# A graph layer on one core: the adds of a gathered pair's sums go to steps 6 and 7 of a block

## The chip, the core and the metric

The kernel runs on one core of a Trainium2 chip. The metric is the time on the device in microseconds (us); lower is better. Times below are of single executions or medians of several, as stated. The engines are called TensorE (PE in the profile, with PEld for its weight loads), VectorE (DVE), ScalarE (ACT), GpSimd (POOL) and SyncE (SP, which issues transfers).

## What is computed

One layer of a graph network over 6250 nodes with 64 features and 206250 edges, which are sorted by their destination:

```python
h = jnp.maximum(_layernorm(x, axis=-1), 0.0)
msg = h[src] + edge_attr_64
agg = jax.ops.segment_sum(msg, dst, num_segments=6250)
y = jax.nn.relu(agg @ W1 + b1) @ W2 + b2
return x + y
```

## The kernel before, in words

All sums `agg` live in one tile on the chip, `sums` in the profile: 128 rows (64 features, in two halves that the first layer's product adds up) and a column for each node. Three things are added into its columns, and then the layers read them.

**Counts.** For most edges `h[src]` isn't fetched. For each destination the kernel counts how often each source occurs, and multiplies the counts with `h`. The nodes are cut into 23 blocks of 252 columns (the last nodes are left to two more sets of layers, 23 and 24), and each block into 14 steps of 6 windows; step n of the whole is step n mod 14 of block n // 14. In a step (`count`) TensorE does 6 products of one-hot tiles (`pc`, line 847) and ScalarE copies them to a ring (`counts`, line 850). The one-hot tiles `hot_lo` and `hot_key` (line 837) are made by VectorE for three steps at once; there are two buffers of each. While block b is counted, the counts of block b - 1 are multiplied with `h` (`pv`, line 866), spread over steps 0 to 6, and `add_products` (line 879) adds them to `sums` at step 10.

**Features of the edges.** `chunk_sum` sums the features of the edges by 48 small products (`bank`, line 434) at steps 7, 10 and 13, from tiles `feat` that SyncE loads two units ahead, into tiles that an earlier sum has freed (line 413); VectorE's one-hot tile for it, `hot` (line 422), is made one step before. Their place among the columns is made by products into `pv` (line 450) at step 3 of the next block.

**Gathered pairs.** The last 18 groups of 1024 edges go another way, two groups at a time, so there are nine pairs, 184 to 200. GpSimd gathers the rows `h[src]` and adds them to the loaded features (`pfeat`, line 296; 16 gathers a pair). When a pair should have landed by the planner's clock, `features_h` sums it by 32 products into `bank` (line 477). A few steps later `place_groups` puts the sums at their columns (`placed`, line 489) and ScalarE copies them to `sum_p` (line 491). Later still `add_sums` adds `sum_p` to `sums` by two VectorE instructions (line 461). The first column is a number that VectorE reads at run time, so the two adds can touch any column: they are ordered against every reader and writer of `sums`.

**Layers.** At step 8 (and 11 where there are enough) `mlp` starts the layers of a block that is complete: `ph` (line 915), the product with W1, in the step itself, with ScalarE's copy `hid` (line 917); `po` (line 922) two steps later, with ScalarE's copy `y` (line 928); the bias onto the rows of `x` (`xs`, line 907) nine steps later, the add to `y` (line 933) ten steps later and the store `out_y` (line 943) on SyncE eleven steps later.

**Checks.** At some steps ScalarE also looks over tiles of indices (`check_nodes`, `check_keys`; `junk` in the profile, line 673): among others at steps 145 and 146 of block 10, and 187 and 188 of block 13.

Each engine's work is written out in order by the Python program: the loop over n calls the work of a step, then what was put down for it with `at`, in the order in which it was put down. Waits between engines are set from the tiles that instructions read and write, in that order. Nothing is scheduled anew behind it.

The step of a pair's adds is found by `add_later`, from the step `n_placed` at which the pair is placed. The steps of the pairs, from the program:

```
pair   summed  placed  adds
184      46      57     62  (block 4, step 6)
186      84      86     91  (block 6, step 7)
188     112     114    119  (block 8, step 7)
190     141     144    149  (block 10, step 9)
192     172     183    188  (block 13, step 6)
194     210     212    217  (block 15, step 7)
196     238     240    245  (block 17, step 7)
198     270     281    286  (block 20, step 6)
200     308     310    313  (block 22, step 5)
```

Of the kernel before, what the change touches and what calls it, by code (L numbers as in the profile page):

```python
# [76 lines left out]
NW = 23  # L77
# [39 lines left out]
def gnn_kernel(ctx: ExitStack, tc: tile.TileContext, x, src_t, dst_t, dst_g, edge, w1, b1, w2, b2, out):  # L117
# [326 lines left out]
    def chunk_place(u):  # L444
        b, c, n = units[u]
        of = by_node.pop(u)
        unplaced[b] -= 1
        for i in range(n):
            a = column(b, (c + i) * CN)
            nc.tensor.matmul(pvs[b][0][i * D:(i + 1) * D, a:a + CN], of[:, i, :], select, start=False, stop=False)  # L450
# [4 lines left out]
    def add_sums():  # L455
        for g, placed in to_add:
            for b in range(GB):
                done_at[g + b] = max(made)
                half = slice(b * D, (b + 1) * D)
                to = agg[half, ds(bases.pop(g + b), W)]  # L460
                nc.vector.tensor_tensor(to, to, placed[half, :], op=OP.add)
        to_add.clear()
# [361 lines left out]
    def count(b, s):  # L824

        t = b * BT + s * ST
        n = b * STEPS + s
        r = n - opens(n)
        if r == 0:
            n = min(ST * (1 if n == 0 else R - 1 if n < R else R), NW * BT - t)  # L830
            assert all(at_col.get(c % KR) == c for c in range(t, t + n)), t
            opened[0] = t + n
            hots[:] = [work.tile([P, R * ST, P], BF16, name="hot_lo"),
                       work.tile([P, R * ST, K + 1], BF16, name="hot_key")]
            for k, (hot, iota_k) in enumerate(zip(hots, (iota_lo, iota_key))):
                m = hot.shape[2] // 2
                nc.vector.tensor_tensor(  # L837
                    hot[:, :n].rearrange("p t (m o) -> p t m o", o=2),
                    iota_k.rearrange("p (m o) -> p m o", o=2).unsqueeze(1).to_broadcast([P, n, m, 2]),
                    keys[:, k, t % KR:t % KR + n, :].unsqueeze(2).to_broadcast([P, n, m, 2]), op=OP.is_equal)  # L840
                if k and 0 < b * STEPS + s < OPEN:
                    nc.vector.memset(spare, 0.0)
        hot_lo, hot_key = (hot[:, r * ST:(r + 1) * ST, :] for hot in hots)
        pc = ps.tile([P, 2, 512], F32, tag="pc", name="pc")
        for j in range(ST):
            k, m = divmod(j, ST // 2)
            nc.tensor.matmul(pc[:, k, m * K:(m + 1) * K], hot_lo[:, j, :], hot_key[:, j, :K],  # L847
                             start=True, stop=True)
        half, i = divmod(s, STEPS // 2)
        nc.scalar.activation(  # L850
            ring[:, (2 * b + half) % 3, :, i * ST * V:(i + 1) * ST * V].rearrange("p h (k m) -> p h k m", k=2),
            pc[:, :, :ST // 2 * K].rearrange("p k (m h) -> p h k m", h=HI), AF.Copy)
# [4 lines left out]
    def multiply(b, upto):  # L857

        if b not in pvs:
            open_pv(b)  # L860
        pv, done = pvs[b]
        assert upto < HI or unplaced[b] == 0
        a, z = sorted(((2 * b) % 3, (2 * b + 1) % 3))
        of = ring[:, a:z + 1:z - a]
        for h in range(done, upto):
            nc.tensor.matmul(pv.rearrange("p (k n) -> p k n", k=2), h2[:, h, :], of[:, :, h, :],  # L866
                             start=(h == 0), stop=(h == HI - 1))
        pvs[b][1] = max(done, upto)
# [3 lines left out]
    def add_products(b):  # L872
        pv, done = pvs.pop(b)[:2]
        assert done == HI
        n = BN - (NX * V if b == SB else 0)
        for a, z in ((0, n),) if 2 * b % 3 != 2 else ((0, NH), (NH, n)):
            to = agg[:, start[b] + a:start[b] + z]
            k = column(b, start[b] + a)
            nc.vector.tensor_tensor(to, to, pv[:, k:k + z - a], op=OP.add)  # L879
        if b == SB:  # L880
            k = column(b, start[b] + n)
            nc.vector.tensor_copy(tail, pv[:, k:k + NX * V])

    def add_seconds(k):
        n = min(4, NX - k)
        node = nc.values_load_multi_w_load_instructions(
            second_n[0:1, k:k + n], engines=[mybir.EngineType.DVE], min_val=0, max_val=DUMP,
            skip_runtime_bounds_check_because="sums of a node's number and 0, at most DUMP by a min")[1]
        for j in range(n):
            to = agg[:, ds(node[j], V)]  # L890
            nc.vector.tensor_tensor(to, to, tail[:, (k + j) * V:(k + j + 1) * V], op=OP.add)
# [4 lines left out]
    def residual(b):  # L896
        if b not in xs:
            xs[b] = late.tile([NP, 2, D], F32, name="xs", bufs=4)
            nc.sync.dma_start(xs[b][:pairs[b]], x[start[b]:start[b + 1], :].rearrange("(p k) d -> p k d", k=2))
# [70 lines left out]
    def pool_until(us):  # L970
        while queue and pool[0] <= us:
            cost, f = queue.pop(0)
            pool[0] += cost
            f()

    def features_h(g):
        read_bases(g, GB)
        sum_groups(g, hot_groups(g), [parts_of.pop(g + b) for b in range(GB)])
        for b in range(GB):
            fetch_h(g + 2 * GB + b)  # L980
# [88 lines left out]
    def clock(n):  # L1069

        return n * HEAD_US if n < STEPS else STEPS * HEAD_US + (n - STEPS) * STEP_US

    steps = [(b, s) for b in range(NW) for s in range(STEPS)]
    first_step = [steps.index((b, 0)) for b in range(NW)]
    last = len(steps)
# [4 lines left out]
    PRODUCTS = (5, 12, 19, 26, 33, 41, HI)  # L1080
    ADDED, LOADED = 10, 2
    LAST, LATE = (5, 10), 9
    GROUPS, PLACED = (0, 1, 2, 4), (1, 2, 4, 5)
    ready = []
    queued = set()
# [2 lines left out]
    def at(step, f, *a):  # L1088
        later.setdefault(step, []).append(lambda: f(*a))

    def mlp(m, n):
        for k, f in ((0, mlp_hidden), (2, mlp_product), (9, bias), (10, mlp_add), (11, mlp_store)):
            at(n + k, f, m)
# [13 lines left out]
    def add_later(n):  # L1107

        upto = h_next

        def f():
            add_sums()
            for m in range(NW, NB):
                if (upto >= G or (start[m + 1] + 30) * (E / N) <= upto * P * J) and m not in queued:
                    queued.add(m)
                    ready.append(m)
        at(n, f)

    for n, (b, s) in enumerate(steps):
        for f in before.get(n, []):  # L1120
            f()
        count(b, s)
        if b >= 1 and s < len(PRODUCTS):
            multiply(b - 1, PRODUCTS[s])
        if b >= 1 and s == PLACES:
            for u in places[b - 1]:
                chunk_place(u)
        if b >= 1 and s == (ADDED if b < NW - 1 else LATE):
            add_products(b - 1)
            if b - 1 > SB:  # L1130
                ready.append(b - 1)
        k = n - (first_step[SB + 1] + ADDED + 1)
        if 0 <= k < 3 * -(-NX // 4) and k % 3 == 0:
            add_seconds(k // 3 * 4)
            if k // 3 == -(-NX // 4) - 1:
                ready[:0] = range(SB + 1)
        if s == LOADED or b == NW - 2 and s == STEPS // 2:
            for m in ready[:len(LAYERS)] if b < NW - 1 else ready + [NW - 2, NW - 1]:
                if m not in xs:
                    residual(m)  # L1140
        if b == NW - 1 and s == STEPS // 2:
            for m in range(NW, NB):
                if m not in queued:
                    residual(m)
        if s in (LAYERS if b < NW - 1 else LAST) and ready and ready[0] in xs:
            mlp(ready.pop(0), n)
        for f in later.pop(n, []):
            f()
        if n >= 3:
            if h_next < G and s in GROUPS and fetched.get(h_next + 1, 1e9) + LAND_US <= clock(n):  # L1150
                features_h(h_next)
                n_placed = next((k for k in range(n + 2, last) if b == NW - 1 or steps[k][1] in PLACED), last)
                at(n_placed, place_groups, h_next)
                h_next += GB
                add_later(next((k for k in range(n_placed + (3 if b == NW - 1 else 5), last) if steps[k][1] != ADDED), last))
            if n == 3:
                pool[0] = clock(n - 1) + OPENING_US
            pool_until(clock(n) + LAND_US)
# [142 lines left out]
```

## Time and profile before

| | |
|---|---|
| three runs without a profile | 478.10, 478.37, 478.75 us; median 478.37 |
| the profiled execution, its own time | 481.19 us |
| its span, first to last instruction | 479.4 us |
| busy: TensorE, VectorE, ScalarE, GpSimd | 418.0, 417.1, 369.0, 355.8 us |

The page and its views are read like this. A row of the order of time has start, length (both us), engine, line, operation, tiles, sizes and number of instructions, and in brackets the engine's idle time before it and what ended that. Neighbouring instructions of the same kind are merged to one row, so a row of 48 products has the length of them all. A row of the table of waits has who waited, for whom, then us in total, times, and the longest. TensorE's granted clock stands in tenths of full speed for 40 equal slices of the span (12 us each), or as a share in a table of stretches. The chain that ended last is followed back from the last instruction, each time to what released it.

### The profile page before, as it was taken

To read this page: it belongs to the slowest core of one execution; us is meant where nothing else is said; L and a number is where in the kernel's file an instruction comes from. 1 tells how busy PE (TensorE), PEld (TensorE's weight loads), DVE (VectorE), ACT (ScalarE), POOL (GpSimd) and SP (SyncE) were. 2 spreads that over 40 slices of the span, in tenths; PEclk is the share of its full clock that TensorE was granted. 3 is DMA by queue.
4 is the path that set the end of the run, shared out by engine and by line. 5 is a ranking of instruction groups with operands and counts; after the bars stand their busy time and mean duration, and the time that the engine had idled before them with its cause. 6 is when DMAs were issued, how large, how long until landed. Compare 5 with 4: busy or idle time off the path is not lost.

```text
span 479.4 us, 17275 instructions
## 1 busy us (share of the span) xinstructions
PE 418.0 (87%) x7339; PEld 373.4 (78%) x7340; DVE 417.1 (87%) x562; ACT 369.0 (77%) x611; POOL 355.8 (74%) x223
## 2 busy tenths in 40 slices
PE   2147698999988999999979999999999999999974
PEld 2136597887887898898878988988988988888964
DVE  7788989889999899989699899898998899898740
ACT  3636889978878789889868789787887788688650
POOL 7777888898888888888888888888888888500000
PEclk9999699999999999999989999999999999999998
DMA  9949457468367668576674694596695694474330
GB/s 236 219 148 313 118 147 167 98 175 218 66 161 193 155 172 228 121 202 166 152 189 114 178 246 105 142 248 142 147 241 123 158 225 106 130 210 133 91 83 16
DMA packets 120050, 77.70 MB, mean 162 GB/s; under 512 B 32448, under 2 KB 118400, under 8 KB 119744
## 3 DMA queue, kind: packets, MB, share of 16 engines
q1 hardware_dynamic: 97452, 67.13, 47.9%
q0 software_dynamic: 22288, 8.67, 14.1%
q8 instruction: 59, 0.97, 0.9%
q10 hardware_dynamic: 228, 0.75, 0.5%
q14 instruction: 23, 0.19, 0.1%
HBM read 72.53 MB, written 3.99 MB: 160 GB/s over the span
## 4 chain that ended last, share of the span: by engine, by line
PE 70%; ACT 11%; DMA 8%; DVE 6%; issue 3%; POOL 1%; DVEq 0%; ACTq 0%; POOLq 0%
PE pv L866 27%; PE pc L847 23%; PE bank L434 10%; ACT counts L850 8%; PE po L922 3%; DMA rows<-in_dst_g,row_i 2%; DMA feat<-in_edge 2%; PE pv L450 2%; DVE hot_key L837 2%; DMA dstq<-in_dst_g,cols_i 2%; DVE hot_lo L837 1%; POOL rows L296 1%; PE ph L915 1%; ACT junk L673 1%; DMA firsts_i<-in_dst_g 1%
## 5 line engine op out<-in xcount | busy, mean ns | idle before, releaser
L296 POOL DMA_INDIRECT pfeat<-table,src_p x144 | 299.7, 2081 | 45.0 <-issue 39.9
L850 ACT ACTIVATE counts<-pc 128x882 fp32r<-128x882 f32 x322 | 286.2, 916 | 56.7 <-PE pc L847 49.9
L847 PE MATMUL pc<-hot_key,hot_lo 128*128 128x147 bf16 x1932 | 180.8, 232 | 27.1 <-ACT counts L850 16.9
L866 PE MATMUL pv<-counts,h 128*128 128x252 f32 x1127 | 171.6, 292 | 0.1
L847 PEld LDWEIGHTS <-hot_lo 128*128 128x128 bf16 x1932 | 132.2, 100 | 49.2 <-issue 22.9
L837 DVE TENSOR_TENSOR hot_key<-iota_key,keys 128x2664 bf16<-128x2664 bf16 (+1 forms) x109 | 165.5, 1519 | 0.0
L837 DVE TENSOR_TENSOR hot_lo<-iota_lo,keys 128x2304 bf16<-128x2304 bf16 (+1 forms) x109 | 145.6, 1336 | 21.4 <-PE pc L847 18.1
L866 PEld LDWEIGHTS pv<-counts,h 128*128 128x128 f32 x1127 | 143.6, 190 | 0.4 <-ACT counts L850 0.3
L434 PE MATMUL bank<-feat,hot 128*21 128x64 f32 x3288 | 62.4, 225 | 0.2 <-DMA feat<-in_edge 0.2
L434 PEld LDWEIGHTS bank<-feat,hot 128*21 128x21 f32 x3288 | 49.9, 103 | 9.5 <-issue 0.7
L422 DVE TENSOR_TENSOR hot<-rel,iota 128x504 f32<-128x504 bf16 x69 | 46.5, 673 | 0.0
L296 POOL DMA_INDIRECT words<-packed,first_i x15 | 21.2, 1413 | 4.6 <-issue 4.3
L296 POOL DMA_INDIRECT rows<-in_dst_g,row_i x15 | 18.7, 1248 | 5.2 <-issue 3.0
L437 ACT ACTIVATE by_node<-bank 128x128 f32<-128x128 f32 x69 | 19.5, 283 | 2.1 <-PE bank L434 1.9
L879 DVE TENSOR_TENSOR sums<-sums,pv 128x126 f32<-128x126 f32 (+2 forms) x31 | 10.0, 343 | 11.0 <-PE pv L866 10.9
L917 ACT ACTIVATE hid<-ph,b1s 128x252 f32<-128x252 f32 (+2 forms) x25 | 11.6, 463 | 9.0 <-PE ph L915 9.0
L922 PE MATMUL po<-w2s,hid 128*126 128x64 f32 (+2 forms) x100 | 17.1, 295 | 1.2 <-ACT hid L917 1.2
L922 PEld LDWEIGHTS po<-w2s,hid 128*126 128x126 f32 (+2 forms) x100 | 13.8, 198 | 4.3 <-ACT hid L917 2.0
L915 PE MATMUL ph<-sums,w1s 128*128 128x252 f32 (+2 forms) x50 | 16.2, 405 | 0.5 <-ACT y L928 0.4
L450 PE MATMUL pv<-select,by_node 128*64 128x42 f32 x274 | 12.6, 235 | 0.0
L450 PEld LDWEIGHTS pv<-select,by_node 128*64 128x64 f32 x274 | 9.9, 137 | 3.1
L312 ACT ACTIVATE inrow<-rows,nhalf 128x256 bf16<-128x256 int32 x15 | 7.4, 499 | 5.2 <-DMA rows<-in_dst_g,row_i 5.2
(201 smaller groups left out, 244.4 us busy)
## 6 DMA issues: line engine op xcount, KB each, us to landing
feat<-in_edge SPq DMA_DIRECT2D x137, 384.0 KB
pfeat<-in_edge SPq DMA_DIRECT2D x18, 256.0 KB
pfeat<-table,src_p POOLq DMA_INDIRECT x144, 4.4
xl<-in_x SPq DMA_DIRECT2D x2, 768.0 KB
xs<-in_x SPq DMA_DIRECT2D x23, 63.0 KB
out_y<-y SPq DMA_DIRECT2D x23, 63.0 KB
dstn<-in_dst_g SPq DMA_DIRECT2D x1, 1024.0 KB
table<-xl SPq DMA_DIRECT2D x1, 800.0 KB
```

Source lines behind the costliest of these rows:

```text
L296: nc.gpsimd.indirect_dma_start(out=rows, out_offset=None, in_=source, in_offset=bass.IndirectOffsetOnAxis(ap=index, axis=0), compute_op=op)
L422: nc.vector.tensor_tensor(hot_of[u][:, :n].rearrange("p c j w -> p (c j) w"), rel[:, c:c + n].rearrange("p c q k -> p (c q k)").unsqueeze( ...
L434: nc.tensor.matmul(bank[q * QP:q * QP + WQ, i * D:(i + 1) * D], hot[:, i, j, :], feat[i][:, j, :], start=(k == 0), stop=(k == JP - 1))
L437: nc.scalar.activation(by_node[u][:, :n].rearrange("p c d -> p (c d)"), bank[:, :n * D], AF.Copy)
L450: nc.tensor.matmul(pvs[b][0][i * D:(i + 1) * D, a:a + CN], of[:, i, :], select, start=False, stop=False)
L837: nc.vector.tensor_tensor(hot[:, :n].rearrange("p t (m o) -> p t m o", o=2), iota_k.rearrange("p (m o) -> p m o", o=2).unsqueeze(1).to_bro ...
L847: nc.tensor.matmul(pc[:, k, m * K:(m + 1) * K], hot_lo[:, j, :], hot_key[:, j, :K], start=True, stop=True)
L850: nc.scalar.activation(ring[:, (2 * b + half) % 3, :, i * ST * V:(i + 1) * ST * V].rearrange("p h (k m) -> p h k m", k=2), pc[:, :, :ST // ...
L866: nc.tensor.matmul(pv.rearrange("p (k n) -> p k n", k=2), h2[:, h, :], of[:, :, h, :], start=(h == 0), stop=(h == HI - 1))
L915: nc.tensor.matmul(ph[:, :n], w1s, agg[:, start[b]:start[b + 1]], start=True, stop=True)
L917: nc.scalar.activation(outs[b][:, :n], ph[:, :n], AF.Relu, bias=b1s)
L922: nc.tensor.matmul(po[:pairs[b], k, :], outs[b][:, k:2 * pairs[b]:2], w2s, start=True, stop=True)
```

## The change

The adds of a pair no longer come five steps behind the placing, at any step but 10. They come at the first step, from three behind the placing on, that is step 6 or 7 of its block. In the last block (22) they still come three steps behind the placing at the earliest, there at any step but 9 (before: but 10).

```diff
     LAST, LATE = (5, 10), 9
+    ADDS = (6, 7)
     GROUPS, PLACED = (0, 1, 2, 4), (1, 2, 4, 5)
...
                 n_placed = next((k for k in range(n + 2, last) if b == NW - 1 or steps[k][1] in PLACED), last)
                 at(n_placed, place_groups, h_next)
                 h_next += GB
-                add_later(next((k for k in range(n_placed + (3 if b == NW - 1 else 5), last) if steps[k][1] != ADDED), last))
+                add_later(next((k for k in range(n_placed + 3, last) if steps[k][1] in ADDS or steps[k][0] == NW - 1 and
+                                steps[k][1] != LATE), last))
```

By it five of the nine pairs get another step: 186 goes from 91 to 90, 188 from 119 to 118, 190 from 149 to 147, 194 from 217 to 216 and 196 from 245 to 244. No instruction is added, taken away or changed, and the order of work on TensorE, ScalarE, GpSimd and SyncE stays the same. On VectorE three places differ. In blocks 8 and 17 the pair's two adds now stand ahead of the add of `y` and `xs` (line 933) that was ahead of them. In block 10 it is this:

```diff
 L933 y<-y,xs                  (step 147)
-L422 hot<-rel,iota            (for the sum of step 150)
 L461 sums<-sums,sum_p   x2
+L422 hot<-rel,iota
 L837 hot_lo, L837 hot_key     (for steps 150 to 152)
 L879 sums<-sums,pv            (step 150)
```

There the two adds were behind `ph` of step 148 in the program and are now ahead of it, so `ph` waits for them where they waited for `ph`.

## The prediction

> **What bounds the kernel now.** I read the page first, then the table of waits, then the placed adds themselves (line 461), then the order of time around the one of them that waits.
>
> ```profile
> span 479.4 us, 17275 instructions
> PEclk9999699999999999999989999999999999999998
> PE 70%; ACT 11%; DMA 8%; DVE 6%; issue 3%; POOL 1%; DVEq 0%; ACTq 0%; POOLq 0%
> ...
> PE pc L847 <- DVE hot_key L837: 5.8, 3, 3.0
> DVE sums L461 <- PE ph L915: 4.4, 1, 4.4
> ...
> L461 DVE TENSOR_TENSOR sums<-sums,sum_p x18: 194/208/211, 122.5 to 447.9; 64x52 f32 x18
> ```
>
> TensorE carries 70% of the chain that ended last, so what makes TensorE stand still sets the time. The waits (us in total, times, longest) hold one pair that belongs together: one of the 18 adds of line 461 kept VectorE idle for 4.4 us until a product of the layers (`ph`, line 915) was done, and TensorE once waited 3.0 us for `hot_key`, which VectorE makes. The row of the granted clock has a dip in its 21st slice, 240 to 252 us. All three are one event, in block 10. First VectorE, with ScalarE's row for the sum that is added:
>
> ```profile
> 233.09 0.21 ACT L491 ACTIVATE sum_p<-placed 128x52 f32<-128x52 f32 x1 [0.23 <-PE placed L489]
> ...
> 233.28 0.28 DVE L933 TENSOR_TENSOR y<-y,xs 126x128 f32<-126x128 f32 x1
> 233.48 0.67 DVE L422 TENSOR_TENSOR hot<-rel,iota 128x504 f32<-128x504 bf16 x1
> 238.54 0.43 DVE L461 TENSOR_TENSOR sums<-sums,sum_p 64x52 f32 x2 [4.39 <-PE ph L915]
> 239.00 1.36 DVE L837 TENSOR_TENSOR hot_lo<-iota_lo,keys 128x2304 bf16<-128x2304 bf16 x1
> 240.27 1.54 DVE L837 TENSOR_TENSOR hot_key<-iota_key,keys 128x2664 bf16<-128x2664 bf16 x1
> ```
>
> `sum_p` was ready at 233.30, yet the adds began at 238.54: their columns of `sums` are known only at run time, so they are ordered behind `ph`, which reads `sums` and stood ahead of them in the program. VectorE works in order, so the one-hot tiles of steps 150 to 152 came that much later. TensorE:
>
> ```profile
> 234.37 0.56 PE L847 MATMUL pc<-hot_key,hot_lo 128*128 128x147 bf16 x6
> ...
> 237.80 0.63 PE L915 MATMUL ph<-sums,w1s 128*128 128x252 f32 x2
> 238.27 0.55 PE L847 MATMUL pc<-hot_key,hot_lo 128*128 128x147 bf16 x6
> 241.87 0.56 PE L847 MATMUL pc<-hot_key,hot_lo 128*128 128x147 bf16 x6 [3.05 <-DVE hot_key L837]
> 242.36 1.37 PE L434 MATMUL bank<-feat,hot 128*21 128x64 f32 x48
> ...
> 246.51 0.55 PE L847 MATMUL pc<-hot_key,hot_lo 128*128 128x147 bf16 x6 [0.33 <-ACT counts L850]
> ...
> 248.16 0.84 PE L866 MATMUL pv<-counts,h 128*128 128x252 f32 x5
> ...
> 239.15:242.56 3.41, 0.69 (x21) 0.57 (x25) 3.41 (x4) 1.22 (x3) 2.80 (x3) 1.00 0.84 214
> 242.56:245.97 3.41, 3.41 (x64) 3.22 (x53) 2.90 (x3) 1.81 (x4) 3.10 (x2) 0.50 0.53 125
> ```
>
> The last two rows are stretches (length, then busy time of PE, PEld, DVE, ACT, POOL, the granted clock, DMA share, GB/s). TensorE was busy for 0.69 of 3.41 us, and in the next 3.41 us its clock was granted at 0.50.
>
> Block 13 is a control: its pair of adds already stands at step 6, ahead of the layers at step 8, and ScalarE has the same two kinds of checks to do just before (`check_nodes` and `check_keys`, steps 145 and 146 here, 187 and 188 there). Its VectorE and TensorE:
>
> ```profile
> 288.36 0.42 DVE L461 TENSOR_TENSOR sums<-sums,sum_p 64x52 f32 x2
> ...
> 293.68 1.54 DVE L837 TENSOR_TENSOR hot_key<-iota_key,keys 128x2664 bf16<-128x2664 bf16 x1
> ...
> 295.13 0.63 PE L915 MATMUL ph<-sums,w1s 128*128 128x252 f32 x2
> 295.60 0.55 PE L847 MATMUL pc<-hot_key,hot_lo 128*128 128x147 bf16 x6
> 296.50 0.55 PE L847 MATMUL pc<-hot_key,hot_lo 128*128 128x147 bf16 x6 [0.35 <-ACT counts L850]
> 296.98 0.87 PE L434 MATMUL bank<-feat,hot 128*21 128x64 f32 x48
> ...
> 299.85 0.55 PE L847 MATMUL pc<-hot_key,hot_lo 128*128 128x147 bf16 x6 [0.61 <-ACT counts L850]
> ...
> 301.49 0.72 PE L866 MATMUL pv<-counts,h 128*128 128x252 f32 x4
> ```
>
> **The change part by part.** Nothing is added or removed. Of the nine pairs of adds, five get an earlier step (91 to 90, 119 to 118, 149 to 147, 217 to 216, 245 to 244). Steps 91 and 217 have nothing of VectorE between old place and new, so the order of work differs for three pairs alone; TensorE, ScalarE, GpSimd and SyncE keep their order.
>
> *The pair of block 10 (149 to 147).* It moves from behind `ph` of step 148 and the `hot` tile to right behind the `y` add that starts at 233.28. That add ends at 233.56, `sum_p` at 233.30, so the pair finds its input ready and needs 0.43 us: until 233.99. `hot` (0.67) follows to 234.66. The next `hot_lo` writes a buffer that the products of step 146 read; these end at 234.37 + 0.56 = 234.93. So `hot_lo` starts at about 234.9 and `hot_key` ends at 234.93 + 1.27 + 1.54 = 237.7 instead of 241.8. TensorE wants it after the products of step 149, which begin at 238.27. In block 13 the two products of the same steps stand 296.50 - 295.60 = 0.90 us apart, held by ScalarE; so TensorE would arrive at 239.17, and `hot_key` is there 1.4 us earlier (in block 13 it ended at 293.68 + 1.54 = 295.22, 1.3 us before its use at 296.50). Nothing is left of the wait. In its place:
>
> - Products of step 149 to those of step 150: 241.87 - 238.27 = 3.60 us now, 0.90 in block 13: **2.70 us gained**.
> - From there to the products two steps later: 246.51 - 241.87 = 4.64 us now, 299.85 - 296.50 = 3.35 in block 13: **1.29 us gained**. This is the slow clock: the 48 small matmuls of line 434 took 1.37 us there and take 0.87 in block 13.
> - From there to the next block: 248.16 - 246.51 = 1.65, against 301.49 - 299.85 = 1.64. Nothing; and 238.27 - 237.80 = 0.47 is the same in both.
>
> Sum 3.99 us. As a cross-check from end to end: 248.16 - 237.80 = 10.36 against 301.49 - 295.13 = 6.36.
>
> The trace halves the clock after a gap of 3.05 us, with 0.69 us of work in the stretch of 3.41 us before the change of clock. The Trainium skill (TensorE: Matmul & The Clock Gate, "HAM oscillation") warns of "PE-idle gaps >~3.4µs" alone; by that length the clock would have stayed full, the sum would be 2.70 and the time 475.7. No longer gap was needed here, so for the profiled execution the measurement decides.
>
> *The new wait.* `ph` of step 148 now waits for the pair. Behind it on TensorE stands everything else of the block. The pair is done at about 234.0, `ph` ran at 237.80: 3.8 us to spare, so the price is zero, and it would be the pair's lateness beyond that.
>
> *Blocks 8 and 17 (119 to 118, 245 to 244).* The pair changes places with the `y` add next to it.
>
> ```profile
> 194.94 0.29 DVE L933 TENSOR_TENSOR y<-y,xs 105x128 f32<-105x128 f32 x1
> 195.15 0.42 DVE L461 TENSOR_TENSOR sums<-sums,sum_p 64x52 f32 x2
> 195.98 1.36 DVE L837 TENSOR_TENSOR hot_lo<-iota_lo,keys 128x2304 bf16<-128x2304 bf16 x1 [0.41 <-PE pc L847]
> ...
> 201.71 0.48 SPq L943 DMA_DIRECT2D out_y<-y  x1
> ...
> 360.37 0.42 DVE L461 TENSOR_TENSOR sums<-sums,sum_p 64x52 f32 x2
> 361.80 1.36 DVE L837 TENSOR_TENSOR hot_lo<-iota_lo,keys 128x2304 bf16<-128x2304 bf16 x1 [1.01 <-PE pc L847]
> ```
>
> The sum of the two is the same, and VectorE then waits 0.41 and 1.01 us for TensorE, so an exchange shows nowhere. In block 8 `y` is ready 0.42 us later, and its store went out at 201.71, some 6 us after it: zero. Without that cover each exchange could cost at most 0.42 us, 0.84 us for both: the far bound.
>
> *What is late next.* From 241.87 on all work on TensorE comes 4 us earlier; GpSimd's gathers don't. The tightest of what it still has to deliver:
>
> ```profile
> 249.30 1.00 POOL L296 DMA_INDIRECT dstq<-in_dst_g,cols_i  x1 [0.30 <-issue]
> 263.98 0.42 DVE L378 TENSOR_SCALAR dstq<-dstq,cols 128x384 f32<-128x384 int32 x1
> ...
> 256.94 1.75 POOL L296 DMA_INDIRECT pfeat<-table,src_p  x1 [0.30 <-issue]
> 272.24 0.65 PE L477 MATMUL bank<-pfeat,hotp 128*21 128x64 f32 x32
> ...
> DMA to landing us min/median/max: 3.0/4.4/10.2
> ```
>
> From issue to use there are 14.7 and 15.3 us; the last row is of all gathers of pairs, at worst 10.2 us to their landing. Less 4 us both still hold.
>
> The profiled execution took 481.19 us, of which 479.4 are the span and 1.8 lie around it: 481.19 - 3.99 = 477.2, with a span of 475.4. The three runs without a profile have a median of 478.37, 2.8 below it. I carry the gain over unchanged: 478.37 - 3.99 = **474.4**.
>
> **The rivals.**
>
> 1. *Only the wait goes, because the runs without a profile had no slow clock.* For: the granted clock is known of the profiled execution alone, which was 2.8 us longer than the median; and the stretch that counted there began 0.3 us into the gap (239.15, after products that ended at 238.82). Cut in the middle of the gap, two such stretches would each hold only half of its 3.05 us, with more work than 0.69 us. Against: the three runs lie within 0.65 us, so they don't mix two cases that are 1.29 us apart. Price: 478.37 - 2.70 = 475.7. The same page of the Trainium skill ("The HAM clock gate") has these windows run free of the kernel, which would let the cut fall anywhere; no run here shows it.
> 2. *The gain is given back or wasn't on the path.* Something that keeps its own time, such as the gathers above, makes TensorE wait for as much later. For: DMA moved 214 GB/s while TensorE stood still, work that must now run beside more of it. Against: the spare times just worked out, and that the loads of features are issued when TensorE frees their tiles, so they move with it. Price: 478.4.
> 3. *Slower: the new wait of `ph` takes the old one's place.* If VectorE reaches the pair late, TensorE, in order, stands at `ph` with all counts behind it. It decides from 3.8 us of lateness, and would have to hold TensorE for 3.99 + 0.96 = 4.95 us to be slower by more than can be told; with the 4.39 us of the old wait back at this place as a hold of TensorE, beside the two exchanges at their bound, 478.37 - 3.99 + 4.39 + 0.84 = 479.6. Against: `sum_p` was there at 233.30, and nothing else holds the pair.
> 4. *The change doesn't do what it says:* the pair still stands behind `ph`. The order of work on VectorE, shown with the change, excludes it; time as rival 2.
>
> **How the numbers follow.** The forecast has 0.56, rival 1 0.29, rival 2 (with 4) 0.06, rival 3 0.04; 0.05 is for a gain larger or smaller than these. The forecast's own range is 474.4 with the spread of the three runs, some 0.4, either way. The range for 8 in 10 goes from 473.6 (twice that spread below the forecast) to 476.6 (rival 1 with the 0.84 of the exchanges). 0.2% is 0.96 us and about what can be told from no change: faster than 477.4 with 0.90, within 0.2% with 0.06, slower with 0.04.
>
> **What would show it.** In the changed profile line 461 has no wait for `ph` any more; the 3.0 us under `pc` from `hot_key` are gone; the PEclk row has no dip at 240 to 252 us; from `ph` of block 10 to the next block's first product it is about 6.4 us instead of 10.36; VectorE waits for TensorE at `hot_lo` near 234.9. The prediction is wrong if `ph` waits for `sums` there, if TensorE's idle time comes back in blocks 11 to 14 at a tile that a gather or a load brings, or if the block shortens while the time does not.

## The result and the profile after

The changed kernel took 474.18 us in the median of nine runs, the kernel before 478.87 in the median of nine, three of which are those that the forecast was made from. The ratio is 0.9907, with an interval of 0.9883 to 0.9931, all of it below 1: faster, by about 0.9%. The forecast of 474.4 (0.9917 of the median it was made from) lies within. All ratios compare fast runs alone, and two profiles of the next section, the first of the one pair alone and the second of all but that pair, are of slow runs, so their block lengths show a direction and not a size.

The profiled execution took 473.48 us. Its page, the row of the span and that of the granted clock:

```profile
span 471.7 us, 17275 instructions
...
PEclk9999899999999999999999999999999999999998
```

The dip in the 21st slice is gone. VectorE of the changed kernel in block 10, in order of time:

```profile
230.38 0.28 DVE L933 TENSOR_TENSOR y<-y,xs 126x128 f32<-126x128 f32 x1
230.58 0.42 DVE L461 TENSOR_TENSOR sums<-sums,sum_p 64x52 f32 x2
231.03 0.68 DVE L422 TENSOR_TENSOR hot<-rel,iota 128x504 f32<-128x504 bf16 x1
232.03 1.36 DVE L837 TENSOR_TENSOR hot_lo<-iota_lo,keys 128x2304 bf16<-128x2304 bf16 x1 [0.32 <-PE pc L847]
233.31 1.54 DVE L837 TENSOR_TENSOR hot_key<-iota_key,keys 128x2664 bf16<-128x2664 bf16 x1
```

The adds follow `y` without a pause, and the only wait left is that of `hot_lo` for a buffer, 0.32 us. TensorE at the same place, up to the first product of block 11:

```profile
234.87 0.63 PE L915 MATMUL ph<-sums,w1s 128*128 128x252 f32 x2
235.34 0.55 PE L847 MATMUL pc<-hot_key,hot_lo 128*128 128x147 bf16 x6
236.24 0.55 PE L847 MATMUL pc<-hot_key,hot_lo 128*128 128x147 bf16 x6 [0.35 <-ACT counts L850]
236.73 0.87 PE L434 MATMUL bank<-feat,hot 128*21 128x64 f32 x48
...
239.59 0.55 PE L847 MATMUL pc<-hot_key,hot_lo 128*128 128x147 bf16 x6 [0.61 <-ACT counts L850]
...
241.24 0.84 PE L866 MATMUL pv<-counts,h 128*128 128x252 f32 x5
```

`ph` waits for nothing. From `ph` to block 11 it is 241.24 - 234.87 = 6.37 us, 10.36 before. The two terms, one by one: 236.24 - 235.34 = 0.90 (3.60 before) and 239.59 - 236.24 = 3.35 (4.64 before).

The span, though, fell by 7.7 us, not by 4. I measured each block from ScalarE's first copy of its counts to that of the next block (us):

```
                   start   block 0  1-9      10      11-21     22 and the end
before             40.65   21.83    163.13   22.77   194.94    36.07
changed            39.11   20.30    163.27   18.78   194.59    35.61
```

Block 10 gives 3.99 us. Another 3.07 come from the start and block 0, before the first instruction that moved (step 90, in block 6); the rest, some 0.7, is spread over the other stretches. Stretches of block 0, before and after (length, busy time of PE, PEld, DVE, ACT, POOL, granted clock, DMA share, GB/s):

```profile
40.65:62.48 21.83, 16.69 (x237) 13.86 (x237) 19.68 (x30) 16.60 (x34) 17.95 (x10) 0.77 0.71 211
```

```profile
39.11:59.41 20.30, 14.47 (x237) 12.31 (x237) 19.24 (x30) 16.31 (x33) 17.86 (x9) 0.92 0.75 227
```

The same instructions ran at a mean clock of 0.77 in the one execution and 0.92 in the other. That is between two executions, not between two kernels; blocks and not spans are compared from here on.

### The profile page after: what moved, and what is told of

The parts are those of the page before. It is cut to its first block, busy times and chain, and to the rows that moved or that the text cites. A ratio compares the mean times of both kernels' runs of the same rounds, so it can differ in the third digit from the quotient of the medians.

```text
span 471.7 us, 17275 instructions
## 1 busy us (share of the span) xinstructions
PE 413.9 (88%) x7339; PEld 370.3 (79%) x7340; DVE 417.1 (88%) x562; ACT 368.3 (78%) x611; POOL 359.7 (76%) x223
## 3 DMA queue, kind: packets, MB, share of 16 engines
HBM read 72.53 MB, written 3.99 MB: 162 GB/s over the span
## 4 chain that ended last, share of the span: by engine, by line
PE 71%; ACT 11%; DMA 5%; DVE 5%; issue 4%; POOL 3%; DVEq 0%; POOLq 0%; ACTq 0%
PE pv L866 27%; PE pc L847 24%; PE bank L434 10%; ACT counts L850 9%; POOL rows L296 3%; PE po L922 3%; PE pv L450 2%; DMA feat<-in_edge 2%; DVE hot_key L837 2%; DMA dstq<-in_dst_g,cols_i 2%; DVE hot_lo L837 1%; PE bank L477 1%; DMA firsts_i<-in_dst_g 1%; PE ph L915 1%; ACT junk L673 1%
## 5 line engine op out<-in xcount | busy, mean ns | idle before, releaser
L847 PE MATMUL pc<-hot_key,hot_lo 128*128 128x147 bf16 x1932 | 178.9, 230 | 25.9 <-ACT counts L850 17.8
L847 PEld LDWEIGHTS <-hot_lo 128*128 128x128 bf16 x1932 | 130.6, 99 | 47.9 <-issue 24.8
L837 DVE TENSOR_TENSOR hot_lo<-iota_lo,keys 128x2304 bf16<-128x2304 bf16 (+1 forms) x109 | 145.7, 1336 | 21.4 <-PE pc L847 18.5
L434 PE MATMUL bank<-feat,hot 128*21 128x64 f32 x3288 | 60.8, 222 | 0.4 <-DMA feat<-in_edge 0.4
L434 PEld LDWEIGHTS bank<-feat,hot 128*21 128x21 f32 x3288 | 48.7, 102 | 9.1 <-DMA feat<-in_edge 0.6
L296 POOL DMA_INDIRECT words<-packed,first_i x15 | 26.4, 1759 | 4.6 <-issue 4.0
L296 POOL DMA_INDIRECT rows<-in_dst_g,row_i x15 | 17.4, 1159 | 4.9 <-issue 3.7
```

Of the source, the lines that this page charges most:

```text
L296: nc.gpsimd.indirect_dma_start(out=rows, out_offset=None, in_=source, in_offset=bass.IndirectOffsetOnAxis(ap=index, axis=0), compute_op=op)
L434: nc.tensor.matmul(bank[q * QP:q * QP + WQ, i * D:(i + 1) * D], hot[:, i, j, :], feat[i][:, j, :], start=(k == 0), stop=(k == JP - 1))
L837: nc.vector.tensor_tensor(hot[:, :n].rearrange("p t (m o) -> p t m o", o=2), iota_k.rearrange("p (m o) -> p m o", o=2).unsqueeze(1).to_bro ...
```

## The experiments

The theory: VectorE, in order, reached the adds while TensorE was still about 4 us of work away from `ph`; that wait, and the slow clock behind TensorE's gap, are the whole gain. The rivals: that the other four pairs carry a part; that a pair behind `ph` has a price of its own; that being ahead of `ph` is what counts; that the slow clock cost nothing.

Four of the kernels ran in two series on chips on which the kernel before took a median of 501 and 502 us, and one of them a third time beside a run of before at 499; there all kernels lost a further 20 us or so all over. Their block lengths are compared with each other and not with the first profiles.

### The one pair alone

```diff
-                add_later(next((k for ...
+                n_add = next((k for ...
+                add_later({190: 147}.get(h_next - GB, n_add))
```

> The kernel before with pair 190's adds alone moved from step 149 to 147. Theory (the whole gain is the wait in block 10): block 10, counted between ScalarE's first copies of counts of two blocks, takes 18.8 us as in the changed kernel (22.8 before), no add of line 461 waits for ph, and the time is that of the changed kernel, about 474.2 (0.990 of before). Rival (the four other pairs carry a part): block 10 shortens as well, but the time stays 1 us or more above the changed kernel's.

> Again, since transfers were disturbed for all kernels of the first series. The kernel before with pair 190's adds alone moved from step 149 to 147. Theory (the whole gain is the wait in block 10): block 10 takes 18.8 us, all other blocks are as before, and the time is that of the changed kernel, 0.990 of before. Rival (the four other pairs carry a part): the ratio stays at 0.993 or more.

Measured: 0.9965 (0.9928 to 1.0003) and, in the second series, 0.9849 (0.9798 to 0.9899) of before, where 0.990 was expected. The two disagree with each other more than the effect is large, so neither settles it alone. Block 10 took 22.93 and 20.05 us, not 18.8. The whole difference between these two lies in the last step before block 11, 4.32 us in the first and 1.43 in the second, behind all that was moved; what held it there stays open. No add waited for `ph`, and from the products of step 149 to those of step 150 it was 0.87 and 0.88 us, as short as in the changed kernel (0.90). TensorE, second series:

```profile
253.66 0.55 PE L847 MATMUL pc<-hot_key,hot_lo 128*128 128x147 bf16 x6
254.54 0.55 PE L847 MATMUL pc<-hot_key,hot_lo 128*128 128x147 bf16 x6 [0.33 <-ACT counts L850]
```

### All but the one pair

```diff
-                add_later(next((k for ... ADDS ...
+                n_add = next((k for ... ADDS ...
+                add_later({190: 149}.get(h_next - GB, n_add))
```

> The changed kernel with pair 190's adds put back to step 149; the four other pairs stay at their new steps. Theory: the wait of some 4.4 us for ph is back, block 10 takes 21.4 to 22.8 us (the lower figure if no slow clock follows the gap), all other blocks are as in the changed kernel, and the time is that of before, 478.4 to 478.9. Rival (the others carry a part): at least 1 us below before.

> Again. The changed kernel with pair 190's adds put back to step 149. Theory: the ratio to before is 1.000 within 0.002; block 10 takes 21.4 to 22.8 us, all others as in the changed kernel. Rival: below 0.997.

Measured: 1.0102 (1.0043 to 1.0162) and 0.9970 (0.9912 to 1.0028) of before; neither lies within the 0.002 of 1 that was expected. Beside the kernel of the section above, with which it shares chip and runs of before, it is slower by a like amount in both series: 0.9965 / 1.0102 = 0.986 and 0.9849 / 0.9970 = 0.988. Block 10 took 28.44 and 26.72 us, above the expected 21.4 to 22.8 and 5.5 and 6.7 more than there, and the wait was back: from the products of step 149 to those of step 150 it was 4.19 and 3.66 us. In order of time, TensorE in the first series and VectorE in the second:

```profile
244.93 0.55 PE L847 MATMUL pc<-hot_key,hot_lo 128*128 128x147 bf16 x6
249.12 0.92 PE L847 MATMUL pc<-hot_key,hot_lo 128*128 128x147 bf16 x6 [3.64 <-DVE hot_key L837]
```

```profile
244.28 0.28 DVE L933 TENSOR_TENSOR y<-y,xs 126x128 f32<-126x128 f32 x1
244.49 0.67 DVE L422 TENSOR_TENSOR hot<-rel,iota 128x504 f32<-128x504 bf16 x1
249.79 0.48 DVE L461 TENSOR_TENSOR sums<-sums,sum_p 64x52 f32 x2 [4.63 <-PE ph L915]
```

So with the four other pairs at their new steps the wait is whole, and with pair 190 alone it is gone. That the other four carry nothing is borne out by the blocks of the changed kernel (163.27 us for blocks 1 to 9, 163.13 before; 194.59 and 194.94 for 11 to 21), to some 0.4 us; the ratios are too wide to add to that. The next two kernels test it more cleanly, on a chip without the loss of 20 us. In both the other four pairs stand at their old steps, and still block 10 took 18.78 us, as in the changed kernel; blocks 1 to 9 took 163.40 and 163.10 us there, and 11 to 21 took 195.02 and 194.61.

### One step earlier or later

```diff
+                add_later({190: 148}.get(h_next - GB, n_add))
```

> The kernel before with pair 190's adds at step 148, the step of ph, ahead of it in the program. Theory: VectorE's order is the same as at 147, so block 10 takes 18.8 us and nothing waits for ph. Rival (ph's new wait for the adds costs something when they come closer to it): ph waits for sums, block 10 over 19.2.

Measured: block 10 took 18.78 us, from `ph` to block 11 it was 6.37, and `ph` waited for nothing; 474.51 us in one run, 477.16 for before beside it. 148 is as good as 147.

```diff
+                add_later({190: 150}.get(h_next - GB, n_add))
```

> The kernel before with pair 190's adds one step later, 150 instead of 149: still behind ph, but behind the one-hot tiles of steps 150 to 152 as well. Theory (VectorE's order and its lead decide, not that the adds stand behind ph): VectorE waits for ph under 1 us, TensorE's wait for hot_key at step 150 is gone, and block 10 takes 18.8 to 19.2 us. Rival (any place behind ph in the block costs the same): a wait of some 4 us, block 10 about 22.8.

Measured: block 10 again 18.78 us, and 474.32 us in one run. VectorE, in order of time:

```profile
233.59 1.54 DVE L837 TENSOR_TENSOR hot_key<-iota_key,keys 128x2664 bf16<-128x2664 bf16 x1
235.04 0.41 DVE L879 TENSOR_TENSOR sums<-sums,pv 128x252 f32<-128x252 f32 x1
235.87 0.43 DVE L461 TENSOR_TENSOR sums<-sums,sum_p 64x52 f32 x2 [0.42 <-PE ph L915]
236.32 0.68 DVE L422 TENSOR_TENSOR hot<-rel,iota 128x504 f32<-128x504 bf16 x1
```

The adds still stand behind `ph`, and still wait for it, but for 0.42 us instead of 4.39: `hot_lo` and `hot_key` of steps 150 to 152 now come first, and when VectorE is through with them TensorE has come to `ph`. One step later is as good as two steps earlier. It was the place between two sets of one-hot tiles that cost 4 us, not the order of adds and `ph`.

### Ahead of ph, but with the input late

```diff
-                at(n_placed, place_groups, h_next)
+                at(147 if h_next == 190 else n_placed, place_groups, h_next)
...
+                add_later({190: 147}.get(h_next - GB, n_add))
```

> The changed kernel with pair 190 placed at step 147 instead of 144, its adds right behind at 147, ahead of ph. Theory (the adds must have their sum_p when VectorE reaches them, 3 to 4 us before TensorE does the same step): VectorE now waits for sum_p instead of ph, some 4.5 us, until about 0.4 us after the place where ph stood; ph waits for the adds up to 1 us, and TensorE then waits about 3 us for hot_key as before: block 10 takes 21.5 to 23 us. Rival (being ahead of ph is what matters): block 10 stays at 18.8 to 19.2.

Measured: block 10 took 23.05 us; one run of 478.97, against 477.16 for before. VectorE and TensorE:

```profile
230.64 0.25 DVE L486 TENSOR_TENSOR sel<-iota_wr,off_p 128x104 f32<-128x104 f32 x1
235.31 0.43 DVE L461 TENSOR_TENSOR sums<-sums,sum_p 64x52 f32 x2 [4.42 <-ACT sum_p L491]
```

```profile
234.02 0.33 PE L489 MATMUL placed<-sel,by_group 128*64 128x52 f32 x4
...
235.88 0.66 PE L915 MATMUL ph<-sums,w1s 128*128 128x252 f32 x2 [1.04 <-DVE sums L461]
236.39 0.55 PE L847 MATMUL pc<-hot_key,hot_lo 128*128 128x147 bf16 x6
239.24 0.91 PE L847 MATMUL pc<-hot_key,hot_lo 128*128 128x147 bf16 x6 [2.30 <-DVE hot_key L837]
240.08 1.49 PE L434 MATMUL bank<-feat,hot 128*21 128x64 f32 x48
```

This is the wait of the prediction's third rival: `ph` stands 1.04 us for the adds, and then TensorE 2.30 us for `hot_key`, and the small products behind it run at 1.49 us for 48, the slow clock again. Being ahead of `ph` is worth nothing if `sum_p` isn't there. In the changed kernel it was placed three steps earlier, and ready before the adds.

### More pairs behind ph

```diff
+                add_later({190: 149, 194: 219, 196: 247}.get(h_next - GB, n_add))
```

> The changed kernel with three pairs behind ph, at step 9 of their blocks: 190 at 149, 194 at 219, 196 at 247. Theory (the price is how far VectorE stands ahead of TensorE where the adds are, less what TensorE still has to do before it needs the next one-hot tile): in blocks 15 and 17 the one-hot tiles of the steps from 9 on were opened at another place, the adds come behind one more set of them, VectorE waits about 2 to 2.5 us and TensorE loses 1.0 to 1.6 us in each; block 10 costs 2.7 to 4.0. Time 4.7 to 7.2 over the changed kernel, about 479 to 481.5. Rival (a pair behind ph has a price of its own, some 4 us wherever it stands): 12 over, about 486. Rival (only block 10 is hurt, by its checks on ScalarE): 4 over, about 478.

> Again. Three pairs behind ph, at 149, 219 and 247. Theory (the price is how far VectorE stands ahead): block 10 takes 21.4 to 22.8 us, blocks 15 and 17 lose 1.0 to 1.6 each against 18.0 and 18.9, with VectorE waiting 2 to 2.5 us in each; 1.004 to 1.007 of before. Rival (4 us for each pair behind ph): blocks 15 and 17 at 22 and 22.9, 1.017.

Measured in the second series: 1.0055 (0.9983 to 1.0127) of before. The first left two runs to compare, 502.8 and 499.7 us, against a median of 494.7 for before, too few for a ratio. Their mean is 1.013 of it, between the theory's 1.004 to 1.007 and the rival's 1.017, so the times don't decide; the blocks do. In both series VectorE waited 1.8 us in block 15 and 2.8 in block 17. Block 10 took 26.70 and 26.10 us, more than expected, as with all but the one pair. Block 17 took 21.14 us twice, and 19.5 to 20.5 in the other kernels of these series; block 15 19.69 and 20.03, and 18.6 to 19.1 in the others. That is a loss of about 0.6 to 1.6 us each and not 4. VectorE and TensorE of block 17, second series:

```profile
379.93 0.68 DVE L422 TENSOR_TENSOR hot<-rel,iota 128x504 f32<-128x504 bf16 x1
383.38 0.45 DVE L461 TENSOR_TENSOR sums<-sums,sum_p 64x52 f32 x2 [2.77 <-PE ph L915]
...
385.52 1.54 DVE L837 TENSOR_TENSOR hot_key<-iota_key,keys 128x2664 bf16<-128x2664 bf16 x1
```

```profile
382.43 0.63 PE L915 MATMUL ph<-sums,w1s 128*128 128x252 f32 x2
382.96 0.56 PE L847 MATMUL pc<-hot_key,hot_lo 128*128 128x147 bf16 x6
384.32 0.55 PE L847 MATMUL pc<-hot_key,hot_lo 128*128 128x147 bf16 x6 [0.80 <-ACT counts L850]
...
387.12 0.96 PE L847 MATMUL pc<-hot_key,hot_lo 128*128 128x147 bf16 x12 [0.85 <-DVE hot_key L837]
```

A set of one-hot tiles covers three steps and is opened at steps that are multiples of three of the whole count. In block 10 TensorE has tiles for one more step behind `ph` (149), in block 17 for two (247 and 248), in block 15 for three (219 to 221), so most of VectorE's wait was covered: 2.77 us there became 0.85 on TensorE.

### The gap filled

```diff
+        if n == 149:
+            fill = ps.tile([P, P], F32, tag="po", name="fill", bufs=1)
+            for _ in range(36):
+                nc.tensor.matmul(fill, onesb, iota_lo, start=True, stop=True)
```

> The kernel before, wait and all, with 36 small products (128 x 128 bf16, result not used) put on TensorE between the counts of steps 149 and 150, where it stands idle; they start when hid has been read, about 0.6 us after the gap begins, and take some 2 us. Theory (the gap also cost 1.29 us by the slow clock that followed): the granted clock stays 1.00 behind it, the 48 products of line 434 take 0.87 us instead of 1.37, and block 10 takes about 21.5 us instead of 22.8. Rival (the slow clock cost nothing, ScalarE would have held TensorE anyway): the clock stays full and block 10 still takes 22.5 or more. Rival (a gap need not be filled, the clock falls for another reason): the clock falls to 0.50 all the same.

> Again. The kernel before with 36 small products on TensorE in the gap. Theory (the slow clock behind the gap cost 1.29 us): clock 1.00 throughout block 10, which takes about 21.5 us; the time is 0.997 of before. Rival (it cost nothing): 22.5 or more and 1.000.

> A third time, for a look that undisturbed blocks stand beside. The kernel before with 36 small products on TensorE in the gap. Theory (the slow clock behind the gap cost 1.29 us of block 10): clock 1.00 throughout block 10, which takes 21.3 to 21.7 us, and VectorE's wait for ph is still 4.4 us. Rival (it cost nothing): 22.5 or more.

Measured: 1.0014 (0.9954 to 1.0075; one more run of that series took 1290 us and is not in the ratio), then 0.9891 (0.9848 to 0.9933) of before, then one run of 495.2 beside 499.0. The 0.997 expected was met by neither ratio. Block 10 took 24.64, 23.33 and 23.73 us. The 21.5 that I had named was not met on these chips, where block 10 without the wait took 20.05 us and more; by the bare length of the block the rival (22.5 or more) would have been right, but with the gap left open the block took 26.10 to 28.44 us in the two series. What can be compared is the stretch behind the gap. In the second series, TensorE with the gap filled, and then with the gap (the kernel with three pairs behind):

```profile
246.48 2.17 PE L1152 MATMUL fill<-iota_lo,onesb 128*128 128x128 bf16 x36 [0.49 <-ACT hid L917]
249.04 0.56 PE L847 MATMUL pc<-hot_key,hot_lo 128*128 128x147 bf16 x6 [0.39 <-DVE hot_key L837]
...
252.83 0.55 PE L847 MATMUL pc<-hot_key,hot_lo 128*128 128x147 bf16 x6 [0.61 <-ACT counts L850]
```

```profile
249.69 0.92 PE L847 MATMUL pc<-hot_key,hot_lo 128*128 128x147 bf16 x6 [3.56 <-DVE hot_key L837]
250.54 1.49 PE L434 MATMUL bank<-feat,hot 128*21 128x64 f32 x48
...
254.81 0.55 PE L847 MATMUL pc<-hot_key,hot_lo 128*128 128x147 bf16 x6 [0.26 <-ACT counts L850]
```

The mean clocks of these two stretches, in the same order:

```profile
249.04:252.83 3.79, 3.00 (x71) 2.50 (x72) 3.79 (x5) 2.44 (x5) 3.10 (x2) 1.00 0.33 53
```

```profile
249.69:254.81 5.12, 4.86 (x71) 4.26 (x71) 3.81 (x5) 2.44 (x5) 4.51 (x3) 0.54 0.43 92
```

The same work took 3.79 us at full clock and 5.12 at a mean of 0.54: 1.33 us, against 1.29 forecast. It was so each time: from the products of step 150 to those of step 153 it was 3.75, 3.79 and 3.64 us in the three runs with the gap filled, and 5.12 in all four with the gap in these series. The granted clock was 1.00 throughout block 10 in all three. The useless products don't shorten VectorE's wait (5.70 us in this run) or the way from step 149 to 150 (3.60 us, as in the first profile of before), they only keep the clock up.

## Why the prediction was right

- *What bounds the kernel* held. The one wait that the tables showed was the one that counted, and the chain through TensorE was shortened by it.
- *The control.* Block 13, whose pair already stood ahead of its layers, gave 6.36 us for the stretch; it became 6.37. Two blocks of one execution with the same work in them predicted to a hundredth what a change of order would do.
- *The time.* That it came out within 0.2 us is in part luck. The kernel before took 478.87 us in the median of nine instead of the 478.37 that I started from, and the timed gain was 4.69 us instead of 3.99; the two nearly cancel. Block 10 itself gave 3.99. (The upper end of the range, 476.6, is 0.1 more than its own sum: 475.67 + 0.84 = 476.51.)
- *The wait, 2.70 us.* 3.60 became 0.90, as worked out. VectorE had been forecast to wait for a buffer before `hot_lo`, and did, for 0.32 us.
- *The slow clock, 1.29 us.* 4.64 became 3.35. Filling the gap showed by itself that the clock falls because of the gap and that it costs about this much (1.33 to 1.48 us on those chips, 5.12 less 3.79 to 3.64). The Trainium skill (TensorE: Matmul & The Clock Gate, "HAM oscillation") warns of gaps over 3.4 us. In the six profiles whose gap was left unfilled it was 2.3 to 3.6 us long, four times under 3.4, and the slow clock followed each time; so the measurement decides.
- *The first rival*, that runs without a profile had no slow clock, is not supported. It turned on where the stretches of 3.41 us cut the gap. They do run free of the kernel, for which the prediction had no run: in the profile of before the clock changes at 51.41, 61.65, 242.56 and 245.97 us, which are 3, 53 and 1 stretches apart, and in the other profiles the cuts fall at other places of the work. But a cut in the middle of the gap didn't keep the clock up. With three pairs behind `ph`, first series, it fell 1.59 us into a gap of 3.06 (246.61 to 249.67):

```profile
244.79:248.20 3.41, 1.54 (x25) 1.18 (x14) 1.83 (x4) 3.24 (x6) 2.97 (x2) 1.00 0.59 133
248.20:251.61 3.41, 1.94 (x50) 1.72 (x54) 3.41 (x4) 1.07 (x2) 2.94 (x2) 0.50 0.57 151
```

TensorE was busy for 1.54 of 3.41 us ahead of the cut, and the slow clock followed, as in every profile that has the wait and no filling. The timed runs came out 4.69 us apart, and their interval, 3.3 to 5.6 us of 478.87, holds 3.99 and leaves 2.70 out; the single runs at 148 and 150, though, came out 2.65 and 2.84 us below the one run of before beside them. What the clock was within block 10 of the runs that were only timed stays open.
- *The new wait of `ph`* was put at zero, with 3.8 us to spare. It was zero at 147 and at 148; with `sum_p` late it was 1.04 us.
- *Blocks 8 and 17* were put at zero and show 19.01 and 18.86 us, 19.00 and 18.86 before.
- *What is late next:* nothing was. Blocks 11 to 21 took 194.59 us, 194.94 before.
- *What I hadn't asked:* whether the adds had to go ahead of `ph` at all. One step later does as much.

## What to carry to other kernels

An engine that works in order and runs ahead of its consumer pays a wait with its lead: the price is not how long the wait is but whether what the consumer needs next stands behind it. So look at what is queued behind a waiting instruction before moving it, and try both directions; here a step later was as good as two earlier. And look for a control within the same profile: here another block with the same work in the wanted order told the gain of the stretch to 0.01 us.

## What the runs showed of the hardware

- A TensorE gap of 2.30 us, behind another of 1.04 (the kernel with the pair placed at 147), was enough for the slow clock, and so was one of 1.81 us (all but the one pair, second series, from 315.35), while one of 1.80 us was not (three pairs behind, first series, from 311.95). What told them apart was how long TensorE was busy in one stretch of 3.41 us: 1.81 us in the stretch from 313.49, 2.31 in that from 309.64, for the gap of 1.80 us was cut in two at 313.05. In the fourteen profiles, from 60 to 460 us, the slow clock followed each of the twelve stretches at full clock with 1.66 us of work or less, and none with more than 1.90; in between it went both ways. On the disturbed chips it lasted up to 10.24 us, 3.41 in the first profile of before.
- The opening's slow clock varies between executions of the same instructions: block 0 took 21.83 us in one and 20.30 in another, 1.5 us that have nothing to do with either kernel.
- On the disturbed chips TensorE stood still within a run of the 48 small products with nothing that the profile shows to wait for, 0.41 us at a time. TensorE with the gap filled, second series:

```profile
242.41 0.88 PE L434 MATMUL bank<-feat,hot 128*21 128x64 f32 x42
243.70 0.30 PE L434 MATMUL bank<-feat,hot 128*21 128x64 f32 x5 [0.41 <-issue]
244.41 0.22 PE L434 MATMUL bank<-feat,hot 128*21 128x64 f32 x1 [0.41 <-issue]
```

What it waited for there no run shows.
